# Stieltjes attention of a sequence run between slots of the window-attention part of the sequences ahead of it

## The chip, the cores and the metric

The kernel runs on one core of a Trainium2 chip. The core has five engines with a queue of instructions each, worked off in order: TensorE (PE, with weight loads shown as PEld), VectorE (DVE), ScalarE (ACT), GpSimd (POOL) and SyncE (SP), which here issues the DMAs. Data lie in SBUF; PE writes to PSUM, eight banks of 128 x 512 floats. The metric is device time in microseconds (us), the median of several runs.

## The reference

Eight sequences of 512 tokens with 128 channels pass through two parts. The first is Stieltjes attention, 16 heads of width 8, causal, applied to the normalized input:

```python
lam = s_masked.max(-1) + 1.0
for _ in range(4):                       # Newton, per row of scores
    d = jnp.maximum(lam[..., None] - s, EPS)
    w = jnp.where(mask, 1 / d, 0.0)
    f, fp = w.sum(-1) - 1.0, -jnp.where(mask, 1 / d**2, 0.0).sum(-1)
    lam = lam - f / fp
p = where(mask, 1 / max(lam - s, EPS), 0);  p = p / p.sum(-1)
x = x + (p @ V) @ Wo.T
```

The second is six layers, each with windowed attention and a feed-forward:

```python
x = attn_layer(shift_tokens(x), ...) + x   # 16 heads of 64; l2-normed, scaled, rotated q, k;
                                           # each token sees its window of 32 and the one before
x = ffn_layer(shift_tokens(x), ...) + x    # LayerNorm, W1, a * gelu(gate), W2
```

The result of the second part is added to its input. Sequences are independent of each other in both parts; layers of one sequence follow each other.

## The kernel before, in words

All arithmetic is in fp32. The program is written through a scheduling layer: the Python program gives instructions and tiles from pools, the layer finds the dependencies, and a scheduler puts the instructions of each engine into a fixed order when the kernel is built. It takes them by their place in the program and by when it expects them to be ready. So each engine's order is fixed before the program runs, and a tile of a pool can be written again only when the last reader of the buffer before has finished.

*First part* (`project` to `attend_end`, L190 to L380). The work of a sequence is 4 batches j (4 heads each, in four groups of 32 partitions) by 4 blocks rb of 128 rows; a block's four pieces a have 32 rows per head and as many keys as the causal mask leaves. `scores` (L237) makes s on PE (L248), and DVE adds the mask, stores it as `ns` and takes the minimum (L253). `newton` (L283) computes 1/(lam + ns) on ACT as Exp(-Ln(.)) (L297, L298; for the two small blocks POOL adds lam first, L263, and L293 takes Ln), DVE takes the sums of 1/d and 1/d^2 from bn_stats (L300) and updates lam with seven small operations (L304 to L315). `attend_add`, `attend_weigh` and `attend_sum` make the final weights, transpose them on PE (L338), mask them on DVE (L341) and multiply by the values (L350). The main loop (L391) treats two blocks at a time, (3, 0) and (2, 1), all four j; it runs Newton for the present pair (`now`), scores for the next and the attention sums for the pair before. Eight PSUM banks belong to this part: four for scores, two for transposes, one for small things and one for the sums. At its end each sequence is written to DRAM (x2) and its normalized transpose stays in SBUF (xT). Then the pools of this part are closed and those of the second are opened.

*Second part* (L428 to L875). One loop over slots t. A slot handles one pair of heads of one sequence in one layer: 8 slots a sequence and layer, 384 in all, in the order layer, sequence, half (four pairs). In slot t the program has `turn` (transposes of q and k, L622, L627), `gather` of the pair three slots back (L680), `turn_weights` of the pair two back (L668), `prepare_qk` for the half ahead (L555 to L581), the exponentials of the pair before, `turn_sums`, `weigh` (scores with the band, L642 to L653), `prepare_v` (L588), one piece of a feed-forward under way, and `leave` (the output product, L708). `spread` (L597) copies v by 18 DMAs from SP into a layout in which each window of 32 rows finds its 64 keys (tile v3, two buffers). PSUM: five banks for most products (tag "mm", pool ps_a), two for scores and sums of the pair (ps_b) and one for the output (ps_c). The feed-forward (L723) is a generator; each `next` gives one stage of it to a slot. Weights of a layer are loaded once and used by all eight sequences.

## Time and profile before

| | |
|---|---|
| runs | 5036.04, 5036.15, 5038.48 us (median 5036.15) |
| profiled execution | 5038.26 us, of which the span is 5036.6 us |
| PE busy | 4208.7 us (84%) |
| DVE busy | 4024.4 us (80%) |
| ACT busy | 3573.7 us (71%) |
| POOL busy | 2990.7 us (59%) |
| first part | about 0 to 1640 us |
| second part | about 1640 to 5036 us |

The page gives busy time by engine over the whole span, which mixes the two parts; the slices and the windows view separate them. A group line reads: line, engine, operation, output and input tiles, shapes, count, then busy time in us and mean duration of one in ns, then idle time of the engine just before them and what ended it. Matmul records overlap, so their busy time is less than count times mean.

### The profile page before, as it was taken

Reading aid. Unit: us, or ns where it says so; the run is one execution under the profiler, and the core shown is the slowest. Engines: PE = TensorE matmul, PEld = TensorE weight load, DVE = VectorE, ACT = ScalarE, POOL = GpSimd, SP = SyncE. Lnnn points to the kernel's source line nnn. Section 1 sums busy time; section 2 is a strip of 40 time slices with the busy share of each in tenths; the row PEclk is TensorE's granted clock in tenths of the full one; section 3 lists DMA queues with packets and bytes.
Section 4 is the critical chain, followed back from the end, with each engine's and each line's share of the span. In section 5 each row is a group of like instructions: output and inputs, shape, how many; then the busy total and the mean of one; then the engine's idle time right before and its main releaser. Section 6 shows DMA issues by size and latency. Waiting matters only on the chain.

```text
span 5036.6 us, 162286 instructions
## 1 busy us (share of the span) xinstructions
PE 4208.7 (84%) x67981; PEld 2476.2 (49%) x67981; DVE 4024.4 (80%) x9484; ACT 3573.7 (71%) x6314; POOL 2990.7 (59%) x3828
## 2 busy tenths in 40 slices
PE   4556566556554999999999999999999999999998
PEld 1233333233323555655556555565555655556554
DVE  7789889889887878777787777777777777777775
ACT  6899999999998566666666666666666666666664
POOL 2444444444445766666666666666666666666663
PEclk7567767667666999999999999999999999999999
DMA  0000000000001323323233232332323323333232
GB/s 9 1 5 1 5 5 1 5 5 1 3 1 31 72 60 68 77 66 68 61 67 85 58 68 64 70 81 56 68 65 78 72 56 71 70 70 77 64 74 48
DMA packets 270480, 240.29 MB, mean 48 GB/s; under 512 B 43920, under 2 KB 265912, under 8 KB 269752
## 3 DMA queue, kind: packets, MB, share of 16 engines
q1 hardware_dynamic: 269752, 229.91, 20.4%
q8 instruction: 539, 8.83, 0.7%
q14 instruction: 189, 1.55, 0.1%
HBM read 21.13 MB, written 4.19 MB: 5 GB/s over the span
## 4 chain that ended last, share of the span: by engine, by line
PE 44%; DVE 25%; ACT 20%; issue 7%; POOL 4%; SPq 0%; DMA 0%; ACTq 0%; POOLq 0%; DVEq 0%
PE m L555 9%; PE po L680 6%; DVE qr L563 6%; DVE stw L300 5%; ACT d L297 5%; PE pT L668 4%; PE acc L708 4%; ACT d L298 4%; PE ptq L622 3%; PE pv L588 3%; DVE ss L561 3%; PE s L642 3%; PE y L779 2%; PE gp L758 2%; PE s L248 2%
## 5 line engine op out<-in xcount | busy, mean ns | idle before, releaser
L569 POOL TENSOR_TENSOR qn<-qr 128x512 f32<-128x512 f32 x768 | 980.3, 1277 | 996.5 <-DVE qr L563 828.2
L563 DVE TENSOR_TENSOR qr<-m,tab 128x1024 f32<-128x1024 f32 x768 | 932.0, 1214 | 0.0
L580 POOL TENSOR_TENSOR qn<-qn,ss 128x512 f32<-128x512 f32 x768 | 787.2, 1046 | 70.5 <-ACT ss L577 70.5
L561 DVE TENSOR_REDUCE ss<-sq 128x8 f32<-128x512 f32 x768 | 522.0, 680 | 376.2 <-ACT sq L560 376.2
L263 POOL TENSOR_TENSOR df<-ns,lam 128x32 f32<-128x32 f32 (+7 forms) x1024 | 397.5, 426 | 606.2 <-DVE lam L315 352.3
L555 PE MATMUL m<-wqkv,xs 128*128 128x512 f32 x1536 | 726.9, 596 | 0.9 <-ACT v L592 0.7
L560 ACT ACTIVATE sq<-m 128x512 f32<-128x512 f32 x768 | 459.8, 599 | 200.9 <-PE m L555 196.1
L297 ACT ACTIVATE d<-ns,lam 128x416 f32<-128x416 f32 (+7 forms) x1024 | 559.5, 616 | 58.7 <-DVE stw L300 29.4
L300 DVE BATCH_NORM_STATS2 stw<-d 128x6 f32<-128x416 f32 (+7 forms) x1024 | 514.3, 561 | 51.8 <-ACT d L298 51.3
L627 ACT COPY qT<-ptq 128x512 f32<-128x512 f32 x768 | 407.9, 582 | 197.2 <-PE ptq L622 197.2
L248 PE MATMUL s<-kn,qj 32*32 32x160 f32 (+15 forms) x4096 | 428.8, 494 | 128.5 <-DVE mn L253 114.9
L338 PE MATMUL dTp<-ident,da 128*128 128x128 f32 x1280 | 291.1, 367 | 292.0 <-issue 67.3
L263 POOL TENSOR_TENSOR da<-ns,lam 128x416 f32<-128x416 f32 (+15 forms) x512 | 311.8, 641 | 288.7 <-PE dTp L338 259.3
L622 PEld LDWEIGHTS ptq<-ident,qn 128*128 128x128 f32 x3072 | 359.6, 141 | 211.3 <-issue 157.5
L588 PE MATMUL pv<-wqkv,xs 128*128 128x512 f32 x768 | 431.6, 644 | 1.1 <-DVE qr L563 0.8
L708 PE MATMUL acc<-oT,wo 128*128 128x512 f32 x768 | 397.7, 599 | 26.7 <-ACT oT L702 26.7
L653 POOL TENSOR_TENSOR pr<-pr,nm 128x512 f32<-128x512 f32 x384 | 401.7, 1046 | 23.5 <-DVE nm L652 20.2
L622 PE MATMUL ptq<-ident,qn 128*128 128x128 f32 x3072 | 399.7, 273 | 6.6 <-POOL qn L580 3.1
L338 PEld LDWEIGHTS dTp<-ident,da 128*128 128x128 f32 x1280 | 195.8, 185 | 419.8 <-issue 199.4
L680 PE MATMUL po<-v,prT 64*32 64x65 f32 x24576 | 378.9, 224 | 22.1 <-DVE pr L647 16.5
L298 ACT ACTIVATE d<-d 128x1856 f32<-128x1856 f32 (+1 forms) x256 | 390.2, 1524 | 0.0
L669 ACT COPY prT<-pT 128x512 f32<-128x512 f32 x384 | 224.7, 585 | 206.7 <-PE pT L668 206.3
(138 smaller groups left out, 7954.2 us busy)
## 6 DMA issues: line engine op xcount, KB each, us to landing
v<-v SPq DMA_DIRECT2D x1152, 130.0 KB
v<-v SPq DMA_DIRECT2D x384, 97.5 KB
v<-v SPq DMA_DIRECT2D x192, 65.0 KB
wqkv<-in_L_ffn_Wqkv_dram SPq DMA_DIRECT2D x24, 256.0 KB
wqkv<-in_L_ffn_Wqkv_dram SPq DMA_DIRECT2D x24, 128.0 KB
wo<-in_L_ffn_Wo_dram SPq DMA_DIRECT2D x12, 256.0 KB
xb<-in_L_attn_x_dram SPq DMA_DIRECT2D x8, 256.0 KB
x<-xb SPq DMA_DIRECT2D x8, 256.0 KB
```

The source lines that it names most:

```text
L263: nc.gpsimd.tensor_tensor(o, n, by.to_broadcast([P, keys(W, a)]), ALU.add)
L297: nc.scalar.activation(dv[a], nv[a], AF.Ln, bias=lam[:, c : c + 1])
L298: nc.scalar.activation(d, d, AF.Exp, scale=-1.0)
L300: nc.vector.bn_stats(st[:, 4 * j + a].rearrange("p u k -> p (u k)"), dv[a])
L555: nc.tensor.matmul(m.rearrange("p h e -> p (h e)"), lhsT=lhsT, rhs=wqkv[:, t, :], start=True, stop=True,)
L561: nc.vector.tensor_reduce(ss[:, t, :], sq, axis=AX.X, op=ALU.add)
L563: nc.vector.tensor_tensor(qr, m.unsqueeze(1).to_broadcast([P, 2, HH, DHL]), tab[:, 2 * t : 2 * t + 2, c, :].unsqueeze(2).to_broadcast([P, ...
L569: nc.gpsimd.tensor_tensor(g["qn"][t][:, c].rearrange("p h (u e) -> p h u e", u=2), halves_of[:, 0], halves_of[:, 1, :, ::-1, :], ALU.add,)
L580: nc.gpsimd.tensor_tensor(qc, qc, ss[:, t, :].unsqueeze(2).to_broadcast([P, HH, DHL]), ALU.mult)
L622: nc.tensor.transpose(pt[:, c * P : (c + 1) * P], g["qn"][t][:, c, 2 * p : 2 * p + 2, :].rearrange("p h e -> p (h e)"), ident,)
L680: nc.tensor.matmul(po[u * QB : (u + 1) * QB, e, c, :], lhsT=prT[rows, c, u * QB : (u + 1) * QB], rhs=g["v3"][rows, n, p, :], start=True, s ...
L708: nc.tensor.matmul(acc, lhsT=wo[:, p, :], rhs=oT, start=(pp == 0), stop=(pp == NPAIR - 1))
```

## The change

The two parts become one program. The first part is a Python generator `stieltjes()` of 528 steps (33 rounds of 16); the loop over slots calls `advance(upto)`, which runs it as far as a goal that grows with the slot number. The second part goes through the sequences in three groups, (0, 1), (2, 3, 4) and (5, 6, 7): all six layers of a group before the next group. A sequence enters the second part (`need`, `enter`) when its first part is done; it reads x2 back from DRAM.

With that come these edits:

- a batch of the first part is one j with all four row blocks, and one batch is in Newton at a time instead of a pair of blocks; q is masked per batch (`mask_q`), ns tiles are turned into the final weights in place;
- pools of both parts are open together: PSUM has two banks for the first part (ps_1), three for "mm" (ps_a), two (ps_b) and one (ps_c);
- q, k and v are prepared per quarter (two pairs) instead of per half: one product m holds q and k of four heads each, one pv tile holds two token blocks; the square goes into the first half of qr; `spread` has 18 DMAs a quarter, of half the size;
- several tiles of the second part have one buffer instead of two (qT, oT2, the feed-forward's tiles share one);
- rotary tables of all layers are computed once, kept in DRAM and loaded per layer; weights are loaded per layer and group;
- in the first group, up to four stages of a feed-forward are given to a slot.

The diff, cut to its core:

```diff
+    groups_of = ((0, 1), (2, 3, 4), (5, 6, 7)) if NB == 8 else (tuple(range(NB)),)
+    units = [(l, b) for grp in groups_of for l in range(DEPTH) for b in grp]
...
-        ps_s = c1.enter_context(tc.tile_pool(name="ps_s", bufs=4, space=PSUM))
-        ps_t = c1.enter_context(tc.tile_pool(name="ps_t", bufs=2, space=PSUM))
-        ps_m = c1.enter_context(tc.tile_pool(name="ps_m", bufs=1, space=PSUM))
-        ps_o = c1.enter_context(tc.tile_pool(name="ps_o", bufs=1, space=PSUM))
...
-    ps_a = ctx.enter_context(tc.tile_pool(name="ps_a", bufs=5, space=PSUM))
+    ps_1 = ctx.enter_context(tc.tile_pool(name="ps_1", bufs=2, space=PSUM))
+    ps_a = ctx.enter_context(tc.tile_pool(name="ps_a", bufs=3, space=PSUM))
...
+    def enter(b):
+        xT[b] = xt_p.tile([P, N], F32, name="xT")
+        normalized_T(fetch(x2[b]), xT[b])
...
+    def evaluate(t, rb):
+        ns, lam = t["ns"][rb], t["lam"]
+        if rb < 2:
+            d = t["df"][rb]
+            nc.scalar.activation(d, d, AF.Ln)
+        else:
+            d = dp.tile([P, width(3)], F32, name="d")[:, 0 : width(rb)]
+            for a, (o, n) in enumerate(zip(pieces(d, rb), pieces(ns, rb))):
+                c = 4 * rb + a
+                nc.scalar.activation(o, n, AF.Ln, bias=lam[:, c : c + 1])
+        nc.scalar.activation(d, d, AF.Exp, scale=-1.0)
+        for a, o in enumerate(pieces(d, rb)):
+            nc.vector.bn_stats(t["st"][:, 4 * rb + a].rearrange("p u k -> p (u k)"), o)
...
+    STEPS = 4 * NUM_ITER
+    def stieltjes():
+        work = [(b, j) for b in range(NB) for j in range(4)]
...
+        for w in range(len(work) + 1):
+            nxt = None
+            if now:
+                first_lam(now)
+            for k in range(NUM_ITER):
+                if now:
+                    now["st"] = sm.tile([P, H, 2, 3], F32, name="stw")
+                    now["df"] = {}
+                    for rb in (1, 0):
+                        now["df"][rb] = d = dp.tile([P, width(rb)], F32, name=f"df{rb}", bufs=1)
+                        add_lam(now, d, rb)
+                    evaluate(now, 3)
...
+                yield
+                if now:
+                    evaluate(now, 2)
+                if before and k == 0:
+                    attend_weigh(before, 3)
+                if k == 0 and w + 1 < len(work):
+                    nxt = open_batch(w + 1)
+                yield
+                if now:
+                    evaluate(now, 1)
+                if before and k in (1, 2):
+                    attend_sum(before, 4 - k)
...
+                yield
+                if now:
+                    evaluate(now, 0)
+                    step(now)
+                if nxt:
+                    for rb in ((), (3,), (2,), (1, 0))[k]:
+                        scores(nxt, rb)
+                yield
+            before, now = now, nxt
+    first = stieltjes()
...
+    def advance(upto):
+        nonlocal done_steps
+        while done_steps < upto:
+            next(first, None)
+            done_steps += 1
+    advance(5 * STEPS)
...
-    wf = ctx.enter_context(tc.tile_pool(name="wf", bufs=2))
-    tp = ctx.enter_context(tc.tile_pool(name="tp", bufs=2))
+    tp = ctx.enter_context(tc.tile_pool(name="tp", bufs=1))
...
+    PQ = 2
+    HQ = 2 * PQ
+        for i, c in enumerate(cs):
+            m = ps_a.tile([P, 2, HQ, DHL], F32, name="m", tag="mm")
+            nc.tensor.matmul(
+                m.rearrange("p t h e -> p t (h e)"), lhsT=xs[:, c * P : (c + 1) * P],
+                rhs=wqkv[:, 0:2, q0 : q0 + HQ * DHL], start=True, stop=True,
+            )
+            qr = ep.tile([P, 2, 2, HQ, DHL], F32, name="qr")
+            sq = qr[:, 0].rearrange("p t h e -> p (t h) e")
...
-    halves = [(l, b, hv) for l in range(DEPTH) for b in range(NB) for hv in range(2)]
+    quarters = [(u, qt) for u in range(len(units)) for qt in range(NS // PQ)]
...
+    def need(b):
+        if b not in entered:
+            advance((4 * b + 5) * STEPS)
+            enter(b)
+            entered.add(b)
...
-        parts = [n for n in parts if next(n, n) is not n]
+        many = 1
+        if last and len(parts) + 1 and units[last["g"]["u"]][1] in groups_of[0] and len(groups_of) > 1:
+            many = 4
+        for _ in range(many):
+            parts = [n for n in parts if next(n, n) is not n]
...
         t += 1
+        u = (t + 6) // NS
+        if u < len(units):
+            need(units[u][1])
+        total = (4 * NB + 1) * STEPS
+        lead = 3 * NS * DEPTH
+        goal = 9 * STEPS + (total - 9 * STEPS) * max(t - NS, 0) // (slots - lead - 2 * NS)
+        if t < NS:
+            goal = 5 * STEPS + 4 * STEPS * (t + 1) // NS
+        advance(min(goal, total))
```

## The prediction

> **What bounds the kernel now.** I read the page's slices first. The program has two parts and the busiest engine changes between them: ACT up to about 1.6 ms, PE after that. In PEclk the reader is to see the granted clock change with the part.
>
> ```profile
> span 5036.6 us, 162286 instructions
> PE   4556566556554999999999999999999999999998
> DVE  7789889889887878777787777777777777777775
> ACT  6899999999998566666666666666666666666664
> PEclk7567767667666999999999999999999999999999
> ```
>
> Then the windows view, one steady stretch of each part and each part whole (columns: PE, PEld, DVE, ACT, POOL busy us, clock, DMA share, GB/s).
>
> ```profile
> 100.00:1500.00 1400.00, 833.98 (x7169) 419.09 (x7169) 1215.95 (x4403) 1303.28 (x1880) 630.43 (x1372) 0.67 0.01 3
> 1750.00:4875.00 3125.00, 3016.72 (x55565) 1851.38 (x55567) 2442.53 (x4142) 1949.25 (x3894) 2105.02 (x2056) 1.00 0.31 69
> 0.00:1640.00 1640.00, 953.88 (x8326) 483.84 (x8326) 1394.89 (x5030) 1481.33 (x2134) 734.46 (x1627) 0.68 0.02 6
> 1640.00:5036.00 3396.00, 3254.85 (x59657) 1992.41 (x59657) 2629.51 (x4454) 2092.40 (x4180) 2256.28 (x2201) 1.00 0.30 68
> ```
>
> In the first part ACT is busy 1303/1400 = 93.1%, DVE 86.9%, PE 59.6%. In the second PE is busy 96.5%, DVE 78.2%, ACT 62.4%. L653 runs once a slot and 358.5 times in that stretch, so a slot lasts 3125/358.5 = 8.72 us and holds 8.42 us of PE, 6.81 of DVE, 5.44 of ACT, 5.87 of POOL.
>
> The timeline of one plain slot shows the order on PE and how long a PSUM bank of m is held: written from 3006.70, the second bank free when the second L563 ends at 3011.93.
>
> ```profile
> 3006.70 1.88 PE L555 MATMUL m<-wqkv,xs 128*128 128x512 f32 x4
> 3008.41 0.60 PE L698 MATMUL po<-ident,o 128*128 128x128 f32 x4
> 3008.99 1.21 DVE L563 TENSOR_TENSOR qr<-m,tab 128x1024 f32<-128x1024 f32 x1
> 3009.11 0.58 ACT L702 COPY oT<-po 128x512 f32<-128x512 f32 x1
> 3009.73 1.12 PE L588 MATMUL pv<-wqkv,xs 128*128 128x512 f32 x2
> 3010.72 1.21 DVE L563 TENSOR_TENSOR qr<-m,tab 128x1024 f32<-128x1024 f32 x1
> ```
>
> Last, the waits of the DMA queue and, from the groups by form, the longest piece of the first part.
>
> ```profile
> SPq L611 <- PE po L680: 1787.0, 94, 23.9
> ...
> L298 ACT ACTIVATE d<-d 128x1856 f32<-128x1856 f32 x128 | 222.5, 1738 | 0.0
> ```
>
> **The change, part by part.** *Work removed: almost none.* Counted in the two programs, Newton (L293 to L315), scores, transposes, q/k preparation and feed-forward have the same numbers and shapes on ACT, DVE and POOL; the value product has the same columns in twice as many matmuls. So the time can only come from overlap, and I price three stages by how far the changed program's instruction order has got. Of the 2048 bn_stats of the first part, 340 stand ahead of the first softmax maximum of the second on DVE, 584 ahead of the eighth, all ahead of the 224th of 384.
>
> *Stage A, start to slot 8* (28.5% of the first part, 8 slots). At today's pace 0.285 x 1640 = 467 us. Two things are added. Only one batch is in Newton instead of two blocks, so nothing else is in Newton while lam is updated: bn_stats of the smallest row block (281+236+209+184 ns) and seven small operations (211+207+206+234+239+203+251 ns) make 2.46 us in which ACT has only the weights of the batch before, 8.7 us a batch. Before slot 1 there are 340/16 = 21 iterations: 0 to 52 us, I take 35, nearer the top since those weights are not ready in every iteration. The 8 slots themselves are hidden (0) or not (8 x 8.72 = 70): ACT has 0.119 x 1481 + 8 x 5.44 = 220 us of work where the first part's pace gives 195, so 28. **A = 530** (467 to 590).
>
> *Stage B, slots 8 to 224* (71.5% of the first part in 216 slots, 0.331% a slot). Per slot DVE has 0.00331 x 1395 + 6.81 = 11.43 us, ACT 4.90 + 5.44 = 10.34, POOL 8.30. PE has 8.42 + 0.00331 x 954 = 11.58 at the clock of the first part. That clock is 0.68 at a PE share of 58%; with PE this full it should be granted 1.00 as in the second part, and the same 128x128 transpose takes 287 ns there (L668) against 367 (L338): 8.42 + 3.16 x 0.78 = 10.88. DVE becomes the bound, with PE 5% and ACT 10% below it. Not overlapped at all, a slot would cost 0.00331 x 1640 + 8.72 = 14.15. No row shows three engines this full, so I bound DVE's share: 93.1% (the busiest engine of today's first part) gives 12.28, 86.9% (DVE there, second in line) gives 13.15. I take the middle, 90%, 12.70, since Newton has slack here (a batch is spread over 9.4 slots, some 119 us, and needs about 51 us alone), and add 0.10 for PSUM: **B = 216 x 12.80 = 2765** (2652 to 3056).
>
> *PSUM* goes from five banks to three for the tiles of the second part (and from eight to two for those of the first). Where this is nothing: in the timeline above pv starts at 3009.73, L702 frees the third bank at 3009.69 and the first L563 one of m at 3010.20. It fits by 0.04 us, so any eviction that is late stops PE. The new DVE order also puts the 0.68 us addition of the band before the second L563. Per slot 0 (it fits) to 1.74 (one eviction behind the longest Exp); 0.10 is nearest to the row above, and the 1.74 is the slower rival's.
>
> *Stage C, slots 224 to 384*: 160 x 8.72, plus 0.10 a slot for PSUM and 0.05 for pv in halves (two more weight loads of 187 ns a slot, beside passes half as long; 0 to 0.4), and 35 us after the last slots as today: **C = 1454** (1430 to 1555).
>
> *DMA and queues.* Spreading v takes 18 DMAs a quarter instead of a half. Each holds SP 0.60 us in the timeline, so 10.9 us in every two slots (17.4 us), SP being 62% busy. The cover is that v3 is free after the gather of slot 2i+4 and read in slot 2i+7, over 25 us at 8.72; SP has no consumer behind it in a hurry, as the 1787 us that it waits for the gather today show. Without cover a quarter would cost some 11 us. Weights and tables are loaded for each of 18 group layers instead of 6, about 220 more DMAs, 0.6 us each on SP, ahead of the quarter that needs them by two slots or more: 0, else some 12 us for each of 15 more layer starts, 180 us. The small loads behind them (x2, xr) have slots of cover.
>
> *Feed-forward of the first group* must end before the same sequence returns two units later. Its chain in rows (sum, shift, two transposes with copies, statistics, gp, gelu with two table loads, ap, y) is about 25 us against 3 to 6 slots of 12.8 us: 0, else one slot for each of 12 units, 150 us.
>
> *Moved setup* (tables, vectors) today lies in a dip: 3396 - 384 x 8.72 = 47 us, of which 35 are the end. The rest, 12 us, is in A's margin.
>
> Sum 530 + 2765 + 1454 = 4749, and 1.7 us around the span (5038.26 less 5036.6), 4751. The profiled execution stands 2.1 us above the median of 5036.15, which changes nothing: **4750 us**, 5.7% less.
>
> **A rule against the row.** The granted clock is the row: 0.68 in the first part, 1.00 in the second. The Trainium skill, "TensorE: Matmul & The Clock Gate", Part 1, says that the clock is gated to half unless the array was busy in a recent window, and that idle gaps bring the half back. By it a stage B full of short PE stalls could stay gated; the row of the mixed stretches says full. With the slow clock PE is the bound at 11.58 and B grows by 216 x (11.58 - 11.43)/0.9 = 36 us. "Perfetto Trace Analysis", Matmuls, asks that independent groups rotate through different PSUM banks, which speaks against three banks; no row here has a price for it.
>
> **The rivals.**
> 1. *Three banks stop PE (slower).* Place: PE's in-order queue in stage B, where an eviction of m stands behind a Newton Exp on ACT. For it: the margin of 0.04 us. Against it: rows of PE wait little for ACT now (0.7 us before all L555). Price: one Exp of 1.74 us on each slot, 12.80 + 1.74 = 14.54, B = 3141, and 0.5 us in C, 80: 5205. It decides from 14.1 us a slot in B, 1.3 us of stall a slot. I give 0.14.
> 2. *The overlap is small.* ACT, DVE and PE each wait for another in fixed orders and a slot costs 13.5 to 14.0: 4900 to 5010. For it: DVE feeds POOL, ACT and PE in turn. 0.16. Within 0.2%: 0.03.
> 3. *DVE fills up.* 95% of 11.43 leaves 12.03, A and C at their low ends: 4500 to 4600. Against it: no stage shows DVE above 87%. 0.15.
> 4. *The change doesn't do what it says*, the first part being run in lumps: advance() is forced by need() to step 144 at slot 2, which is why A holds 28.5%; a second lump at slot 106 holds 128 bn_stats, 6%. Both are in the counts. If more were serial, rival 2's price holds.
>
> **How the numbers follow.** The forecast (4600 to 4900) has 0.52, rival 3 0.15, rival 2 0.16, no change 0.03, rival 1 0.14. 0.2% is about what a measurement of this kernel can tell from no change. So faster 0.83, same 0.03, slower 0.14. The range 4560 to 5060 leaves out the better half of rival 3's tail and most of rival 1. The forecast's own range is 4600 to 4900.
>
> **What would show it.** Eight slots done by about 530 us; then a stretch to about 3300 us in which DVE is near 90%, PE near 85%, ACT near 80%, clock 1.00; then slots of 8.9 us. DVE at 80% with PE waiting for "qr" or "ns" in stage B is rival 1. Wrong by more: a clock under 0.8 in B, slots of C over 9.5 us, or PE waiting for v3 DMAs.

## The result, and the profile after

The changed kernel takes 5064.4 us (median; 5060.53 to 5068.51) where the kernel before, run beside it, takes 5037.3. The ratio is 1.0054 with a 95% interval of 1.0036 to 1.0071: slower, by half a per cent, where 4750 us was forecast. The miss is 314 us, and it is not in one place.

The page of the changed kernel, slices of 127 us:

```profile
span 5066.8 us, 166956 instructions
PE   4556598888888887798888888888999999989998
DVE  6678688988888998888898999888777777777775
ACT  6777677777777777767777877778555555555554
PEclk6667699999999998899999999999999999999999
```

The three stages of the prediction are all there. The eighth softmax maximum of the second part (L658) starts at 652.6 us, the 224th at 3508.3. The windows view with these borders (columns: PE, PEld, DVE, ACT, POOL busy us, clock, DMA share, GB/s):

```profile
0.00:653.00 653.00, 349.36 (x3409) 176.00 (x3409) 477.21 (x1555) 467.96 (x699) 275.34 (x570) 0.68 0.08 23
653.00:3508.00 2855.00, 2456.84 (x39774) 1463.48 (x39772) 2528.57 (x6001) 2162.28 (x3844) 1767.27 (x2329) 0.96 0.24 57
3508.00:5066.00 1558.00, 1401.42 (x25568) 902.47 (x25568) 1128.25 (x1906) 885.23 (x1758) 937.47 (x924) 0.99 0.30 72
```

| stage | forecast us | measured us | difference |
|---|---|---|---|
| A, start to slot 8 | 530 | 653 | +123 |
| B, slots 8 to 224 | 2765 (12.80 a slot) | 2856 (13.22 a slot) | +91 |
| C, slot 224 to the end | 1454 | 1558 (9.46 a slot, 45 behind the last) | +104 |

In B the shares are nearly those forecast (DVE 2528.57/2855 = 88.6%, PE 86.1%, ACT 75.7%, clock 0.96, where 90, 85, 80% and 1.00 were named), though each holds more work: DVE 2528.57/216 = 11.71 us a slot where the sum had 11.43, PE 11.37 where it had 10.88. A and C are the surprise: in A no engine is near full (ACT 71.7%, DVE 73.1%, against 90.3% and 85.1% in the whole first part before), and C, which has nothing of the first part in it, runs slots of 9.46 us where the last 160 slots of the kernel before take 8.66 each.

In A the chain of Newton shows in the timeline, one iteration of the batch in Newton. ACT's last Exp of the iteration ends at 234.98 and its next Ln starts at 240.31:

```profile
234.51 0.47 ACT L282 ACTIVATE df<-df 128x320 f32<-128x320 f32 x1
234.77 1.73 DVE L284 BATCH_NORM_STATS2 stw<-d 128x6 f32<-128x288 f32 x4
236.42 1.76 DVE L284 BATCH_NORM_STATS2 stw<-df 128x6 f32<-128x160 f32 x8
238.09 0.54 DVE L319 TENSOR_TENSOR dT<-dTp,seen 128x384 f32<-128x384 f32 x1
238.55 0.19 DVE L290 TENSOR_TENSOR s<-stw 128x32 f32<-128x32 f32 x1
238.66 0.55 DVE L319 TENSOR_TENSOR dT<-dTp,seen 128x384 f32<-128x384 f32 x1
...
240.10 0.18 DVE L299 SCALAR_TENSOR_TENSOR lam<-sw,lam 128x16 f32<-128x16 f32 x1
240.31 1.20 ACT L281 ACTIVATE d<-ns,lam 128x416 f32<-128x416 f32 x2 [5.34 <-DVE lam L299]
```

When ACT is through, DVE has the bn_stats of three row blocks still before it (twelve instructions, 3.4 us), and two maskings of the batch before stand among the seven small operations, one ahead of the first and one behind it. ACT waits 5.34 us; I had priced 2.46.

In C, a plain slot of the timeline, m to m in 4000.30 to 4008.00:

```profile
4000.30 1.88 PE L563 MATMUL m<-wqkv,xs 128*128 128x512 f32 x4
4002.02 0.60 PE L700 MATMUL po<-ident,o 128*128 128x128 f32 x4
4002.77 0.62 ACT L665 ACTIVATE pr<-pr 128x512 f32<-128x512 f32 x1
4003.29 0.58 ACT L704 COPY oT<-po 128x512 f32<-128x512 f32 x1
4003.92 1.13 PE L600 MATMUL pv<-wqkv,xs 128*128 128x256 f32 x4 [0.52 <-ACT oT L704]
...
4008.00 1.88 PE L563 MATMUL m<-wqkv,xs 128*128 128x512 f32 x4
```

Two banks hold m, the third holds po3 until L704 has copied it, and pv has to wait for that copy. The copy itself stands behind the Exp of the next pair (L665), which before the change came after it. The waits view says how often, in stage C:

```profile
PEld pv L600 <- ACT oT L704: 78.3, 117, 0.7
PE pv L600 <- ACT oT L704: 59.4, 117, 0.6
```

### The profile page after: what moved, and what is told of

Its sections match the earlier page's. It is cut to its first block, busy times and chain, and to the rows that moved or that the text cites. A ratio compares the mean times of both kernels' runs of the same rounds, so it can differ in the third digit from the quotient of the medians.

```text
span 5066.8 us, 166956 instructions
## 1 busy us (share of the span) xinstructions
PE 4207.6 (83%) x68749; PEld 2541.9 (50%) x68749; DVE 4134.0 (82%) x9460; ACT 3515.5 (69%) x6298; POOL 2980.1 (59%) x3821
## 5 line engine op out<-in xcount | busy, mean ns | idle before, releaser
L563 PE MATMUL m<-wqkv,xs 128*128 128x512 f32 x1536 | 772.1, 619 | 63.6 <-ACT qT L634 42.5
L572 DVE TENSOR_REDUCE ss<-qr 128x8 f32<-128x512 f32 x768 | 515.4, 677 | 291.5 <-ACT qr L569 290.1
L264 POOL TENSOR_TENSOR df<-ns,lam 128x160 f32<-128x160 f32 (+7 forms) x1024 | 398.8, 427 | 393.2 <-DVE lam L299 337.3
L569 ACT ACTIVATE qr<-m 128x512 f32<-128x512 f32 x768 | 455.3, 599 | 208.4 <-PE m L563 203.2
L600 PE MATMUL pv<-wqkv,xs 128*128 128x256 f32 x1536 | 447.9, 414 | 166.2 <-ACT oT L704 105.1
L603 ACT COPY v<-pv 128x512 f32<-128x512 f32 x384 | 225.1, 586 | 310.9 <-PE pv L600 193.1
L252 PE MATMUL s<-kn,qj 32*32 32x416 f32 (+15 forms) x4096 | 375.0, 446 | 72.7 <-DVE mn L256 62.3
L316 PE MATMUL dTp<-ident,ns 128*128 128x128 f32 x1280 | 253.6, 310 | 189.9 <-POOL ns L264 84.3
L563 PEld LDWEIGHTS m<-wqkv,xs 128*128 128x128 f32 x1536 | 264.5, 196 | 260.4 <-issue 133.8
L600 PEld LDWEIGHTS pv<-wqkv,xs 128*128 128x128 f32 x1536 | 266.3, 194 | 254.2 <-ACT oT L704 149.0
```

Of the source, the lines that this page charges most:

```text
L563: nc.tensor.matmul(m.rearrange("p t h e -> p t (h e)"), lhsT=xs[:, c * P : (c + 1) * P], rhs=wqkv[:, 0:2, q0 : q0 + HQ * DHL], start=True, ...
L569: marks["act"] = nc.scalar.activation(sq, m.rearrange("p t h e -> p (t h) e"), AF.Square)
L572: nc.vector.tensor_reduce(ss[:, i, :], sq, axis=AX.X, op=ALU.add)
L600: nc.tensor.matmul(pv[:, i], lhsT=xs[:, c * P : (c + 1) * P], rhs=cols, start=True, stop=True,)
```

## The experiments

Sixteen kernels were run, each beside the kernel before. "Slot 8" is the start of the eighth softmax maximum, B and C are us per slot from there to the 224th and from the 224th to the last, from one profiled execution each. The expectations reckon with marks later in a slot, the copy of prT (665 us for slot 8 of the changed kernel), the sums behind it (671) or the copy of oT (676; 13.26 and 9.36 us a slot); where that bears on a verdict, the text gives the time at that mark.

| kernel | us | ratio to before (95%) | slot 8 at | B | C |
|---|---|---|---|---|---|
| before | 5037.3 | | | | 8.66 |
| changed | 5064.4 | 1.0054 (1.0036–1.0071) | 653 | 13.22 | 9.46 |
| 1 first part whole, ahead | 5743.2 (one run) | | | 9.48 | 9.34 |
| 2 before, with three banks | 5358.3 | 1.0633 (1.0615–1.0651) | | 9.50 | 9.47 |
| 3 five banks in C | 4990.9 | 0.9905 (0.9891–0.9920) | 654 | 13.21 | 8.99 |
| 4 Newton step in halves in A | 5012.5 | 0.9947 (0.9933–0.9962) | 596 | 13.26 | 9.42 |
| 5 Exp behind the copy of oT | 5046.1 | 1.0019 (1.0009–1.0028) | 653 | 13.25 | 9.33 |
| 6 = 3 + 4 | 4942.0 | 0.9810 (0.9794–0.9826) | 597 | 13.25 | 8.99 |
| 7 = 3 + 4 + 5 | 4921.8 | 0.9770 (0.9755–0.9785) | 592 | 13.20 | 8.95 |
| 8 four banks and one | 5185.4 | 1.0294 (1.0278–1.0309) | 771 | 13.49 | 9.06 |
| 9 nine batch times ahead of slot 1 | 5087.1 | 1.0101 (1.0086–1.0116) | 682 | 13.17 | 9.42 |
| 10 one more DVE operation for each slot | 5111.0 | 1.0146 (1.0131–1.0161) | 682 | 13.30 | 9.44 |
| 11 = 7, part of the step on POOL | 4961.0 | 0.9853 (0.9836–0.9869) | 592 | 13.38 | 8.95 |
| 12 four more transposes a slot | 5198.6 | 1.0321 (1.0304–1.0338) | 652 | 13.53 | 9.86 |
| 13 one more copy on ACT a slot | 5080.4 | 1.0082 (1.0067–1.0097) | 656 | 13.29 | 9.39 |
| 14 five banks for both parts | 5128.7 | 1.0177 (1.0162–1.0193) | 642 | 13.94 | 8.93 |
| 15 = 14 + 4 + 5 | 5071.3 | 1.0066 (1.0051–1.0081) | 599 | 13.94 | 8.85 |
| 16 = 7, halves for all batches | 4911.9 | 0.9747 (0.9731–0.9763) | 593 | 13.19 | 8.94 |

### Stage A: the chain of lam

**1. The whole first part ahead of the second.**

```diff
-    advance(5 * STEPS)
+    advance((4 * NB + 1) * STEPS)
```

> The changed kernel, but the whole first part (five groups, still one chain of batches at a time) runs ahead of the first slot: it prices the single chain with nothing of the second part in it. Stage A of the changed kernel took 665 us where I had summed 530. Theory 'the chain is exposed' (each Newton iteration of a batch waits for lam of the one before, 4 to 5 us of it and not 2.46): the first part, 1640 us long before, comes to 2000 to 2200 us, and stage A is the same 665 us up to the point at which the ninth batch ends. Rival 'slots and loads mixed into stage A made it long': the first part stays at 1640 to 1750 us. The 384 slots behind it go by the price of three banks: 9.3 to 9.5 us each if the slots after number 224 of the changed kernel are slow by themselves, 8.7 to 8.8 if they are slow for what stood ahead of them. In all 5650 to 5850 us by the first of each, 5050 to 5200 by the second.

The windows view of it, the stretch that corresponds to stage A and the slots:

```profile
0.00:604.00 604.00, 278.59 (x2358) 131.20 (x2358) 417.77 (x1462) 427.08 (x602) 218.97 (x515) 0.64 0.06 18
2200.00:5600.00 3400.00, 3089.78 (x56716) 2001.20 (x56715) 2494.49 (x4169) 1952.80 (x3927) 2118.37 (x2075) 0.99 0.31 75
```

The first part's last product comes at 2075 us instead of 1640, and the 584 bn_stats that I counted ahead of the eighth slot are done at 604 us, with no slot beside them. ACT is busy 427/604 = 71% there. So the chain alone is most of stage A: 137 us more than the 467 of the pace before, 3.8 us for each of 584/16 = 36.5 iterations. The first part as a whole and the total lie where the first theory put them, but it had stage A at the full 665 us without the slots, and so left them nothing. The waits are the ones of the timeline; the groups of the first part's Ln, first here, then in the kernel before (busy us, mean ns, idle before it and what ended it):

```profile
L281 ACT ACTIVATE d<-ns,lam 128x416 f32<-128x416 f32 (+7 forms) x1024 | 559.2, 617 | 456.8 <-DVE lam L299 308.0 <-DVE lam L270 148.7
```

```profile
L297 ACT ACTIVATE d<-ns,lam 128x416 f32<-128x416 f32 (+7 forms) x1024 | 559.5, 616 | 58.7 <-DVE stw L300 29.4 <-DVE lam L315 18.9 <-DVE lam L271 10.3
```

The same Ln waits 457 us in place of 59. That difference, 398 us, is nearly all of the 435 by which the first part is longer. The first part also has two PSUM banks where it had eight; kernel 14 below, with five for both parts, has slot 8 only 11 us earlier, which speaks against a large share of the banks in the 137.

**4. The Newton step in halves for the first nine batches**: lam and its sums get two tiles, one for row blocks 3 and 2, one for 1 and 0, and the first half is stepped before the small blocks are evaluated.

```diff
-            lam=sm.tile([P, H], F32, name="lam")
+            lam=[sm.tile([P, H // 2], F32, name=f"lam{i}") for i in range(2)]   # first nine batches
...
                 if now:
                     evaluate(now, 1)
...
+                    if len(now["lam"]) == 2:
+                        step(now, 1)
...
                     evaluate(now, 0)
-                    step(now)
+                    step(now, 0)
```

> The changed kernel, with the Newton step of the first nine batches in two halves of eight columns each, with tiles of their own, so that the Ln of the next iteration's first row blocks need not wait for the step on the last ones. It adds small DVE instructions in stage A and changes nothing behind it. Theory 'the chain is exposed': ACT's waits for lam in stage A (33 + 80 us of its 186 idle us) go down by most of their length, and stage A falls from 665 to 550 to 590 us, the whole to 4950 to 4995 us. Rival 'stage A is bound by something else (the rstd, stats and POOL steps at the ends of batches, the loads)': stage A 640 to 665 us, the whole 5035 to 5070 us. Stages B and C the same by both.

Slot 8 comes at 596 us, 57 earlier, and the whole is 52 us shorter. That is the direction of the first theory and less than it gave: at the expectation's mark slot 8 comes at 612 us where 550 to 590 was named, and the whole is 18 us above its range. The rival, no change, is further off. ACT's waits for lam in stage A (lines 291, 312 and 281 are the former 281, 299 and 270) are cut to a third; they had been 79.9 and 33.0 us:

```profile
ACT d L291 <- DVE lam L312: 25.5, 16, 3.1
...
ACT d L291 <- DVE lam L281: 10.6, 2, 10.3
```

**9. All nine batch times ahead of the first slot** (`advance(5 * STEPS)` becomes `advance(9 * STEPS)`).

> The changed kernel, but the first nine steps' worth of batches (five in the change) run ahead of the first slot, so that no slot lies in stage A. With the whole first part ahead, the same point of it was reached at 604 us; in the changed kernel, with 8 slots beside it, slot 8 is done at 670 us. Theory 'the 8 slots are not hidden in stage A: the chain of lam and the slots take turns': slot 8 at 660 to 685 us again, the whole within 15 us of the changed kernel, 5050 to 5080 us. Rival 'most of the 8 slots is hidden (28 us of 70, as I had it), and the chain is what became longer': slot 8 at 695 to 715 us, the whole 25 to 45 us longer, 5090 to 5110 us.

Slot 8 starts at 682 us, 29 later than in the changed kernel. At the mark by which that kernel stands at 671 it is 701 here, which is in the rival's range and not in that of the first theory; the whole is 23 us longer, just short of the rival's 25. The slots took 682 - 604 = 78 us here and 653 - 604 = 49 in the changed kernel, so 29 us of them are hidden in stage A and 49 are not. I had left 28 unhidden. So the rival is right that part of the slots is hidden, but it is less than half and not most.

### Stage C: three banks

**2. The kernel before with three banks in place of five** (`bufs=5` becomes `bufs=3` for ps_a, nothing else).

> The kernel before with one number changed: three PSUM banks for the pool of the attention slots instead of five. Its slots take 8.77 us each with five; the changed kernel's, with three, take 9.375 where nothing of the first part runs beside them. Theory 'three banks alone': 384 slots of 9.3 to 9.5 us, 200 to 270 us slower, a ratio of 1.04 to 1.055. Theory 'three banks, and the exponential of pr put ahead of the copy of oT on ACT, together' (before, the copy stands ahead of the exponential): 0 to 0.15 us for a slot, 0 to 60 us in all, a ratio of 1.00 to 1.012. The first part uses the pool too, for the m products, and may lose up to 30 us by either.

This is the plainest result of the study: 320 us, 6.3%, for one number, more than either theory. Over the same stretch of the second part that the prediction showed for five banks, PE is busy 2871.31/3125 = 91.9% where it had been 96.5%:

```profile
1750.00:4875.00 3125.00, 2871.31 (x50911) 1686.25 (x50909) 2236.60 (x3788) 1799.37 (x3564) 1927.65 (x1882) 0.99 0.28 63
```

A slot takes 9.50 us where it took 8.70, with ACT in the old order and nothing of the first part beside it. PE's waits in that stretch are for evictions at several places, not at one; none of these three rows stands in the same view of the kernel before:

```profile
PEld po L698 <- ACT v L592: 112.1, 83, 2.5
PE po L698 <- DVE qr L563: 107.7, 82, 1.7
PEld m L555 <- ACT prT L669: 89.0, 124, 0.9
```

**3. po3 and pv2 from the first part's banks once that has ended**, which makes five for stage C.

```diff
-        pv = ps_a.tile([P, 2, 2, PQ * DHL], F32, name="pv2", tag="mm")
+        pool, tag = bank()
+        pv = pool.tile([P, 2, 2, PQ * DHL], F32, name="pv2", tag=tag)
...
+    def bank():
+        return (ps_1, "p1") if done_steps >= (4 * NB + 1) * STEPS else (ps_a, "mm")
```

> The changed kernel, with po3 and pv2 taken from the banks of the first part once that has ended, so that the last 160 slots have five banks again; ACT's order stays, the exponential ahead of the copy of oT. Theory 'banks' (pv of the next pair waits for the bank that the copy of oT frees, 108 such waits of 0.5 to 0.7 us in 144 slots): these slots fall from 9.375 to 8.7 to 8.9 us, 75 to 110 us less in all, about 4960 to 4990 us, a ratio of 0.985 to 0.992 against the kernel before. Rival 'the order on ACT alone, or pv in two halves, costs it': the slots stay at 9.2 to 9.4 us and the time at 5035 to 5065 us. Stages A and B the same by both (665 and 2835 us).

A slot of C falls from 9.46 to 8.99 and the time by 73 us, at the lower edge of the first theory's 75 to 110, while A and B stay (654 us, 13.21). Of the 117 waits of pv for oT 5 are left:

```profile
PEld pv L601 <- ACT oT L706: 3.4, 5, 0.7
PE pv L601 <- ACT oT L706: 2.6, 5, 0.5
```

This one edit makes the change faster than the kernel before, by one per cent. What is left, 8.99 against 8.66, was not taken apart: pv in two halves and tiles with one buffer are in it, and a wait that the kernel before does not have, of ACT's copy of v for the transfers of spread (65 us in all in stage C of the changed kernel, 64 here).

**5. The Exp behind the copy of oT on ACT**, as before the change, with three banks.

```diff
-        if 1 <= t < len(pairs) + (0 if a else 1):
-            exponentials(pairs[t - 1])
         gelus()
         if last:
             turn_sums(last)
+        if 1 <= t < len(pairs) + (0 if a else 1):
+            exponentials(pairs[t - 1])
```

In `turn_sums` the copy of oT becomes the instruction that the Exp must follow.

> The changed kernel with three banks, but with the exponential of pr put back behind the copy of oT on ACT, as before the change, in all 384 slots. The kernel before with three banks has taken 9.52 us for a slot in that order, the changed kernel 9.375 (9.46 with its first part ahead) in the order exponential first. Theory 'three banks, whatever the order on ACT': the wait of pv for the copy of oT goes (72 and 55 us in 144 slots), and another wait on a bank takes its place: slots of 9.3 to 9.5 us after number 224, the whole within 5045 to 5100 us. Theory 'the order, together with three banks' (which I held until the run of three banks alone): slots of 8.8 to 8.9 us, the whole at 4960 to 4990 us.

PE's own wait of that kind in stage C all but goes, from 59.4 us to:

```profile
PE pv L600 <- ACT oT L704: 0.8, 3, 0.3
```

Yet the slot gains only 0.13 us: other idle time takes its place (PE's wait of po for o, L692, goes from 28.4 to 42.3 us), and the time is 18 us shorter, not 75, at the foot of the first theory's range and far from the second's. The order on ACT was visible in the trace and was not the main cause; the number of banks was.

**6 and 7. Together.**

> Both: the Newton step of the first nine batches in two halves, and po3 and pv2 in the first part's banks once that has ended. If the two losses lie in stages of their own (A: -52 us of the whole, C: -73 us), they add: 4925 to 4950 us, a ratio of 0.977 to 0.983 against the kernel before. If one gives back what the other gains (the slots that come earlier meet the same end of the chain of batches), 4960 to 4990 us.

> The same two, and the exponential of pr behind the copy of oT. Where the order on ACT matters at three banks (stage B, 216 slots with 45 and 64 us of PE and its weight loads waiting for oT), 20 to 60 us less than without it, 4875 to 4920 us; where three banks cost the same in any order and five banks hide either, within 15 us of the kernel with the two alone.

The two losses lie in stages of their own and add: 52 and 73 us separately, 122 together. The order on ACT gives 20 us more, at the foot of its range.

**8. Four banks for the slots and one for the first part.**

```diff
-    ps_1 = ctx.enter_context(tc.tile_pool(name="ps_1", bufs=2, space=PSUM))
-    ps_a = ctx.enter_context(tc.tile_pool(name="ps_a", bufs=3, space=PSUM))
+    ps_1 = ctx.enter_context(tc.tile_pool(name="ps_1", bufs=1, space=PSUM))
+    ps_a = ctx.enter_context(tc.tile_pool(name="ps_a", bufs=4, space=PSUM))
```

> The changed kernel with four banks for the slots and one for the first part (three and two in the change). Theory 'three banks cost 0.5 to 0.6 us for each slot of stage C and the chain wants its two': stage C falls by 60 to 90 us (8.8 to 9.0 us for a slot), stage A, where the products s, the transposes dTp and po now share one bank, grows by 30 to 100 us, and stage B by 0 to 150 us: 5030 to 5230 us. Rival 'the chain's bank count matters little, since its length is in lam': stage A stays at 665 us, stage B gains up to 0.3 us for a slot, 4920 to 4990 us.

C falls to 9.06, nearly as with five, but A grows by 118 us, more than expected, and B by 0.27 us a slot. The chain needs its second bank more than the slots need their fourth.

### Stage B: what sets a slot of 13.2 us

I had DVE as the bound. Seven kernels tried this.

**10. One more DVE operation**, written into each slot, with no consumer:

```diff
+        most = tp.tile([P, 2, NT], F32, name="most")
+        nc.vector.tensor_reduce(most, band.unsqueeze(1).to_broadcast([P, 2, NT, KB]), axis=AX.X, op=ALU.max)
```

> The changed kernel with one more DVE instruction in each of the 384 slots, a maximum over 512 elements of a constant, whose result nobody reads (0.68 us, by the row of the same reduction). It asks what sets stage B, where DVE is busy 88.5%. Theory 'DVE sets stage B': slots 8 to 224 grow by 0.6 to 0.77 us each (13.1 to 13.8), 130 to 165 us; in stage C, where PE and the banks set the slot and DVE is busy 74%, 0 to 0.3 us a slot, 0 to 50 us. In all 5190 to 5280 us. Rival 'the three banks and the waits between engines set stage B, DVE has 11% of room': 0 to 0.35 us a slot in B, 5070 to 5160 us.

The kernel does not run what the expectation says. An instruction whose result nobody reads and that reads only a constant can stand anywhere in DVE's order, and the scheduler put all 384 far ahead of their slots. The windows view of L658, the new reduction (its busy time and count, clock, DMA share, GB/s):

```profile
0.00:682.00 682.00, 176.24 (x261) 0.68 0.08 22
682.00:1543.00 861.00, 82.95 (x123) 0.96 0.24 59
1543.00:5111.00 3568.00, 0.00 (x0) 0.97 0.26 63
```

So 261 of them run in stage A, which explains why 30 of the 47 us that the whole got longer lie there. The other 123 run in the first 65 slots of stage B, 1.28 us a slot; from slot 73 on there are none, and the slot is as long as in the changed kernel (13.32 us in both). In those 65 slots it lasts 13.25 us where it lasted 12.99, a fifth of what was added, with DVE busy 816.81/861 = 94.9%:

```profile
682.00:1543.00 861.00, 743.13 (x11956) 440.84 (x11954) 816.81 (x1897) 647.18 (x1149) 524.69 (x687) 0.96 0.24 59
```

DVE has room in stage B, then, for work that may run at any time. What an instruction costs that has its place in the slot's chain, this run does not tell, and the price of 0.07 us for 0.68 that an expectation below takes from it is not one.

**12 and 13. More on PE and on ACT**: the four transposes of the weights made twice, and the copy of prT made twice. Here each added instruction writes what a later one of the slot reads, and it stands in its slot.

```diff
             nc.tensor.transpose(pT[:, c, :], pr[:, c].rearrange("p e k -> p (e k)"), ident)
+            nc.tensor.transpose(pT[:, c, :], pr[:, c].rearrange("p e k -> p (e k)"), ident)
...
         nc.scalar.copy(prT, pT)
+        nc.scalar.copy(prT, pT)
```

> The changed kernel with the four transposes of the weights (pT) made twice in each slot, into the same bank: 4 x 0.28 = 1.1 us more PE work, beside the weight loads. In stage B a slot lasts 13.26 us (from the copy of oT of slot 8 to that of slot 224), in stage C 9.36. Theory 'PE sets stage B, DVE's share being high by chance': +0.8 to 1.1 us a slot in B, 170 to 240 us, and as much in C, 130 to 180 us: 5360 to 5480 us. Theory 'no engine's busy time sets stage B, but the order of waits between the two parts (banks, lam, evictions)': 0.1 to 0.5 us a slot in B, 20 to 110 us, and 0.6 to 1.1 in C, 100 to 180 us: 5180 to 5350 us.

> The changed kernel with the copy of prT made twice in each slot, 0.59 us more on ACT, which also keeps the bank of pT for that much longer. Theory 'ACT sets stage B' (its evictions stand behind Newton's Ln and Exp): +0.45 to 0.7 us a slot in B, 100 to 150 us; in C, where three banks bind and the bank is kept longer, 0 to 0.4 us, 0 to 60 us: 5165 to 5275 us. Theory 'no single engine': 0 to 0.25 us a slot in B, 5065 to 5180 us.

The added PE work is less than the 1.1 us that the expectation prices. The eight transposes, 0.27 us each, start 0.11 us apart:

```profile
4006.95 0.27 PE L673 MATMUL pT<-ident,pr 128*128 128x128 f32 x1
4007.05 0.27 PE L672 MATMUL pT<-ident,pr 128*128 128x128 f32 x1
4007.16 0.27 PE L673 MATMUL pT<-ident,pr 128*128 128x128 f32 x1
```

By the windows view of pT the second four add 0.49 us of PE's time to a slot of stage B and 0.45 in stage C. The slot grows by 0.31 and 0.40, so most of it is paid. Stage B is some 67 us longer, and PE is busy 67 us more in it than the 2456.84 of the changed kernel; PE's idle time, 398 us, stays as it was:

```profile
652.00:3575.00 2923.00, 2524.25 (x40633) 1566.06 (x40621) 2555.32 (x5997) 2164.55 (x3843) 1765.60 (x2330) 0.96 0.23 55
```

The second copy adds (2266.37 - 2162.28)/216 = 0.48 us of ACT's time to a slot of stage B and costs 0.07:

```profile
656.00:3526.00 2870.00, 2490.37 (x39733) 1471.18 (x39726) 2534.61 (x6002) 2266.37 (x4060) 1766.90 (x2332) 0.95 0.23 56
```

So ACT does not set stage B. Both additions stand in the same chain, from the weights to their sums, so the length of that chain isn't what the transposes cost. Of the three engines PE, which is not the busiest, is the one whose time a slot pays for. That PE's work alone sets the slot is not shown: PE is idle for 1.84 us of the 13.22.

**14 and 15. One pool of five banks for both parts** (ps_1 goes, ps_a has five buffers, all tiles have the tag "mm").

> The changed kernel with one pool of five banks in place of two and three: both parts draw on all five in turn. In stage C, where the first part has ended, this is five banks again: 8.9 us a slot instead of 9.36, 75 us less. In stage B: theory 'the split of the banks sets B' (PE waits for the eviction of one of three): 12.3 to 12.9 us a slot instead of 13.26, 80 to 200 us less, 4790 to 4910 us in all. Theory 'the banks matter little in B': 13.1 to 13.4 us, 4960 to 5020 us. A worse outcome is that the buffers, taken in turn, hold up a slot behind a Newton product: 13.5 us and more, over 5020 us.

> One pool of five banks, the Newton step of the first nine batches in halves, and the exponential behind the copy of oT. If the banks are what sets stage B, 4720 to 4850 us; if they matter little there, the same as the kernel with po3 and pv2 in the first part's banks, 4900 to 4960 us; if the buffers taken in turn hold up the slots, over 4980 us.

C is cured (8.93, 8.85), but B gets worse by 0.7 us a slot, the worse outcome that the expectations name. The waits view of the first of them, stage B, beside the same of the changed kernel, shows the attention sums of the first part, for whose dT the PE queue now stands still four to seven times as long:

```profile
PEld po L327 <- DVE dT L318: 196.0, 84, 7.4
PE po L327 <- DVE dT L318: 178.3, 85, 7.2
```

```profile
PEld po L328 <- DVE dT L319: 45.4, 48, 3.9
PE po L328 <- DVE dT L319: 26.1, 28, 3.7
```

PE's wait alone grew by 178.3 - 26.1 = 152 us, 0.70 us a slot, which is nearly the whole 0.72: the slot grew by what PE waited. Whether the scheduler's order for one pool or the turn of the buffers makes PE stand there was not tested. So these two runs do not tell whether the split into two and three banks holds B at 13.2. It stays a candidate: in stage B of the changed kernel PE waits 45.0 us for the copy of oT and 30.4 for qr ahead of pv, and 39.2 for the copy of qT ahead of m, three evictions, 0.53 us a slot together.

**11 and 16. The chain in stage B**, both from kernel 7: in 11 two of the seven small operations of a step move to POOL for the batches of stage B, in 16 the step is in halves for all batches (`SPLIT` from 9 to 32).

```diff
+        eng = nc.gpsimd if len(t["lam"]) == 1 else nc.vector
-        nc.vector.tensor_tensor(s1, mean, st[:, :, :, 0], ALU.mult)
+        eng.tensor_tensor(s1, mean, st[:, :, :, 0], ALU.mult)
         q2 = st[:, :, :, 0]
-        nc.vector.tensor_tensor(q2, s1, mean, ALU.mult)
+        eng.tensor_tensor(q2, s1, mean, ALU.mult)
```

> The kernel of split chains in stage A, po3 and pv2 in the first part's banks at the end and the exponential behind oT (4921.76 us), with two of the seven small operations of the Newton step (the two products over 128 x 32, 0.44 and 0.40 us on DVE) on POOL for the batches of stage B. It takes 0.84 us from DVE for each of some 92 iterations in B, 77 us, adds about as much or twice that to POOL (62% busy there), and puts two changes of engine into each iteration of the chain. Theory 'DVE sets stage B and the chain has room there' (a batch takes 62 us alone and is spread over some 120 us): 40 to 80 us less, 4840 to 4885 us. Rival 'the chain or the waits between engines set it': no change or up to 60 us longer, 4915 to 4985 us.

> The fastest kernel so far (4921.76 us: halves of the Newton step for nine batches, po3 and pv2 in the first part's banks at the end, the exponential behind oT), with the Newton step in halves for all 32 batches. A slot of stage B takes 13.24 us there. It adds seven small DVE instructions to each of some 92 iterations of stage B, 7 x 0.25 = 1.8 us, 0.75 us a slot, and lets the Ln of the next iteration start before the last row blocks are through. Theory 'the chain of lam still sets part of stage B': its shortening outweighs the work, 12.8 to 13.15 us a slot, 20 to 95 us less, 4825 to 4900 us. Theory 'the chain has room in stage B': by the price of an extra DVE instruction (0.07 us for 0.68) 13.25 to 13.4 us, 4920 to 4960 us; by DVE's full price 14.0, 5080 us.

Less work on DVE and a longer chain: 0.18 us a slot worse, as the rival had it; ACT's waits for lam from 700 to 3400 us go from 78 us in kernel 7 to 113. More work on DVE and a shorter chain: no worse, 13.19 instead of 13.20, between the two theories; ACT's waits for lam fall to 68, with DVE at 2512.30/2700 = 93.0% where it was 2384.20/2700 = 88.3%. First kernel 16, then kernel 7:

```profile
700.00:3400.00 2700.00, 2332.37 (x37770) 1404.15 (x37771) 2512.30 (x6376) 2063.14 (x3654) 1674.58 (x2212) 0.95 0.24 57
```

```profile
700.00:3400.00 2700.00, 2329.84 (x37441) 1385.41 (x37440) 2384.20 (x5668) 2054.60 (x3629) 1673.07 (x2219) 0.95 0.24 56
```

So a longer chain does reach stage B, and DVE's busy time is not its limit: it is 84.7% in 11, 88.3% in 7 and 93.0% in 16, for slots of 13.38, 13.20 and 13.19 us. Both runs change the chain and DVE's work at once, so neither has a price of its own. 4911.9 us is the fastest kernel of the study, 2.5% faster than the one before the change.

## Why the prediction was wrong

**The view of stages held.** The borders that the counts of the instruction order gave are those of the trace, the clock in the mixed stage is nearly full (0.96, so the half clock did not come), and the waits for the transfers of the extra weights come to under 5 us in stages A and B together. The lump of rival 4 is there as counted: between the sixth softmax maximum at 495 us and the seventh at 644 there is none. Rival 3, DVE filling up, did not come. What failed are terms of the sum, all in the same direction.

**"Before slot 1 there are 340/16 = 21 iterations: 0 to 52 us, I take 35"** measured 137 (kernel 1). Two things were wrong in it. The gap: I priced the bn_stats of the smallest block and the seven operations as if DVE were idle when ACT ends; DVE is behind by the statistics of two more blocks, and other work stands between the seven operations. An iteration costs 3.8 us more over the stage, and the one gap shown is 5.34. And the count: 21 iterations stand ahead of the first slot, but the stage runs to the eighth, 36.5 of them. That is 102 of the 123 us of stage A. The other 21 are the slots: 49 unhidden, where I took 28.

**"I take the middle, 90%, 12.70"** for stage B. The share came out at 88.6% and the slot at 13.22, inside the bounds of the prediction, but the reason given, that DVE is the bound, is refuted: DVE is 93.0% busy in slots of the same length (kernel 16) and 94.9% in slots of 13.25 us (kernel 10), while the slot pays for most of the work added to PE, which the prediction had 5% below DVE. That the share came out near was luck, and part of the 0.42 us a slot that B is longer than forecast is plain work, the 11.71 us of DVE and 11.37 of PE in place of 11.43 and 10.88; the rest was not separated. Rival 2, "ACT, DVE and PE each wait for another in fixed orders", describes it better, though the slot is below its 13.5 us. The runs show that a slot of B pays for work added to PE, that longer waits of PE (kernel 14) and a longer chain lengthen it, and that ACT and DVE have room; which waits of PE could go stays open. Taken in turn, by kernel 1, the two kinds of work in a slot are (2075 - 604)/216 + 9.48 = 16.3 us, so the overlap does hide 3.1 us a slot. But 14.1 is what the old first part and five banks would give in turn, and against that it is only 0.9: most of what the overlap hides is what the change itself added.

**"Per slot 0 (it fits) to 1.74 (one eviction behind the longest Exp); 0.10 is nearest to the row above"**, for three banks, measured 0.80 us in the kernel before (kernel 2) and 0.47 in stage C of the changed one (kernel 3). The row above was one plain slot: "It fits by 0.04 us". In stage C of the changed kernel pv waits 117 times in 160 slots; and kernel 5, in which it fits again, is hardly faster, because PE then waits elsewhere. One margin in one slot does not price a pool. Stage C has 77 us from it (1558 against 1481 in kernel 3) where the sum had 16, which is 61 of its 104. "Perfetto Trace Analysis", Matmuls, in the Trainium skill, which asks that independent groups rotate through different banks so that evictions overlap the next products, pointed the right way; the prediction let it go for want of a row, and kernel 2 would have been that row.

**The rest of C**, 43 us (1481 in kernel 3 against 1454 - 16 without the term for PSUM), is 8.99 for a slot where 8.72 and 0.05 for pv in halves were taken, and 42 us behind the last slot for 35. pv in halves, the single buffers and the transfers of v, which I had at nothing, may all be in it; it was not separated.

**Rival 1 had the right resource in the wrong place.** It set the price on stage B, behind a Newton Exp; the 77 us that were measured lie in stage C, where there is no Newton at all. In stage B the price was not measured, since with both parts open there are no more banks to give; the waits named under kernels 14 and 15 say that it need not be nothing.

The sign, too, follows from this: either loss alone decides it. With five banks in C the ratio is 0.9905, with a shorter chain in A 0.9947, with both 0.9810.

## What to carry to other kernels

Overlapping two parts makes them share what each had for itself; price that first, by running the old kernel with the smaller share (here three banks in place of five, +6.3%) and the new first part with nothing beside it (+435 us). The stage with two parts in it was not priced by the busy share of its busiest engine; adding work to each engine in turn told more. Such an addition must write what a later instruction of the slot reads, or the scheduler moves it away (kernel 10), and what it adds is read from the trace and not from its length (kernel 12). And a gap in a chain was as long here as the backlog of the engine that closes it, not as the instructions of the last link.

## What the runs showed of the hardware

The clock in the profile's rows can be far from what the durations of the matmuls show. In kernel 8 it reads 0.97 from 50 to 200 us and 0.50 from 200 to 400 us (windows view, last three columns clock, DMA share, GB/s):

```profile
50.00:200.00 150.00, 66.87 (x459) 22.23 (x455) 91.92 (x314) 105.53 (x148) 49.72 (x111) 0.97 0.00 1
200.00:400.00 200.00, 105.20 (x671) 41.11 (x669) 120.47 (x414) 118.34 (x169) 51.56 (x114) 0.50 0.02 5
```

The same transposes, dTp, take 437 ns in the first stretch and 440 in the second (groups of PE, mean ns behind the busy time):

```profile
L316 PE MATMUL dTp<-ident,ns 128*128 128x128 f32 x59 | 17.9, 437 | 49.2 <-POOL ns L264 32.7 <-DVE dT L319 12.4 <-DVE mn L256 2.6
...
L316 PE MATMUL dTp<-ident,ns 128*128 128x128 f32 x103 | 33.1, 440 | 33.3 <-DVE dT L319 24.8 <-DVE mn L256 3.1 <-ACT d L281 1.6
```

In the changed kernel they take 296 ns in stage B (1000 to 3000 us), where the clock reads 0.96. So the durations do not follow the reading: 437 ns at 0.97 is nothing like the 296 at 0.96. Why it reads 0.97 there was not looked into. A clock is better read together with the duration of a matmul that runs throughout.

The prices of added work were the other surprise. In slots of 13.2 us with DVE 88.6%, PE 86.1% and ACT 75.7% busy, 0.49 us more of PE's time cost 0.31 us and 0.48 us more of ACT's cost 0.07; the busiest of the three took 1.28 us of work without a fixed place for 0.26.
